# One stream of steps through four attentions, with the first block of the masked attention cut in two by its keys

## The chip, the cores and the metric

The kernel runs on one core of one Trainium2 chip. The metric is the device time of one execution in microseconds (us), lower is better. The profile is of one more execution of the same program.

## The reference

Two transformer layers run one after the other on x, 2048 rows of 256, with 16 heads of 16. The first layer has two attentions and an MLP, the second a masked self-attention, an attention over a context of 1601 rows, and an MLP. Cut to the order of the four attentions:

```python
# layer 0 (mod_*: LayerNorm, then scale and shift), x0, x1 = halves of 1024 rows
x0 = x0 + g * mha(mod(ln(x0)));   x1 = x1 + g * mha(mod(ln(x1)))        # stage 0
ox = attend(q(x0), k(x1), v(x1)); oy = attend(q(x1), k(x0), v(x0))      # stage 1
x = x + g * concat(ox @ w, oy @ w)
x = x + g * gelu_mlp(mod(ln(x)))
# layer 1
x = ln(x + mha(x, x, x, mask))       # stage 2: all 2048 keys, int mask 2048 x 2048
x = ln(x + mha(x, ctx, ctx))         # stage 3: 1601 keys
x = ln(x + relu_mlp(x))
```

Every softmax subtracts the row's maximum. Stage 2 needs keys of every row of x, so of every row that the first layer's MLP has finished.

## The kernel before

**Blocks, groups, units, steps.** The queries are tiled in 4 blocks of 512 rows, the heads in 4 groups of 4. A unit is (stage, block, group): 16 units a stage, 64 in all. The keys of a group lie in two slots (`kT[g][slot]`, `V[g][slot]`), each with half of the keys. Stages 0 and 1 use one slot for a block, stages 2 and 3 both. Blocks go in the order of `ORDER`: 0, 1, 2, 3 in stage 0, and 2, 3, 0, 1 in the others. In stage 2 slot 0 holds the keys of blocks 2 and 3, slot 1 those of blocks 0 and 1.

A unit has two phases. The maxima (`maxima`, L812) multiply queries by keys with queries on the partitions, and VectorE takes row maxima: with one reduction (L827), in stage 2 with two instructions that add the mask and reduce (L820). `negated` and `as_rows` turn the maxima into a row layout (L851, L856). The weights (`weights_of`) compute the transposed scores (L872), add the negated maxima through a small matmul (L879), in stage 2 also the transposed mask (L887), and ScalarE takes the exponential (L892). `values_of` (L908) multiplies by V, whose column of ones gives the sums of the weights. A step is one exponential: 16 a unit in stages 0 and 1, 32 in stage 2, 26 in stage 3.

**The stream.** `stream(stages)` emits all instructions; each engine runs its own in the order of emission. In each step it emits some maxima of the next unit (4 tiles ahead), one pair of values, one step of weights, and then `after(step)`: small tasks from `later` that are due, a mask transpose (`mask_columns`, L780), one key or value transfer from `transfers`, and one advance of the first generator in `background`. At step 2 of a unit, `copy_sums` (L940 to L948) takes the sums of the unit before; `invert` and `divide` (L958 to L973) follow 4 and 8 steps later. When the last group of a block is done, `chain_after` puts the block's chain into `background`, to begin 9 steps on.

**Chains.** `chain_cross(b)` is the longest: projection (L455), LayerNorm, transposes (L339), 8 up products (L509), GELU (L523), 8 down products (L531), transposes, keys (L381), values (L411), queries (L381). Its keys and values go through DRAM, and from there into `kT` and `V` (L701, L715). `chain_context(n)` turns a part of the context into keys and values of stage 3. A generator's piece that needs a PSUM bank is held back in a step in which something in `later` is due or soon will be, or a mask transpose was made or will be made in the next step. `ensure` advances the background generators, with nothing between them, until what is asked for has been emitted.

**The end of stage 1.** The program calls

```python
    stream((0, 1))
    background += [[chain_context(n), 0, False] for n in range(NB)]
    stream((2, 3))
```

The first call finishes the last chain of stage 1, `chain_cross(1)`, with no attention around it, before the second begins with the 32 maxima of its first unit. In that chain the mask of the first masked block is loaded and turned to bf16 (`mask_rows`, L768, L769), in buffers of the tag `w_mlp`.

Of the kernel before, what the change touches and what calls it, by code (L numbers as in the profile page):

```python
# [11 lines left out]
F32 = mybir.dt.float32  # L12
# [39 lines left out]
CTX = ((0, 512), (512, 384), (896, 512), (1408, 193))  # L52
EB = 5
WB = 5
HB = 8
AHEAD = 4
COLUMNS = 6
# [16 lines left out]
def two_layers(ctx: ExitStack, tc: tile.TileContext, a: dict, out: bass.AP):  # L74
# [70 lines left out]
    ident = sb.tile([P, P], F32, tag="ident", name="ident")  # L145
    make_identity(nc, ident)
# [4 lines left out]
    identR = sb.tile([P, P], F32R, tag="identR", name="identR")  # L151
    nc.vector.tensor_copy(identR, ident)
# [103 lines left out]
    cols = sb.tile([P, 48], F32, tag="cols", name="cols")  # L256
    nc.sync.dma_start(cols, a["cols"])
# [327 lines left out]
    def chain_cross(b):  # L585

        last = b == ORDER[1][-1]
        t = residual(x_in(b))
        yield from project(1, b, gated(rows["a1"], t, b))
        if last:  # L590
            load_output(2)
            rows["a2"] = load_rows(7, 3)
        yield 3
        xn = stage([P, TPB, D], name="xn")
        yield from normalize(xn, t, 1e-6)
        hT = yield from transposed(xn, mod=(2, b // 2))

        q0 = ORDER[2][0]
        if last:
            mask_rows(q0, 0)  # L600
        yield from mlp(
            mlp0, 32, AF.Gelu_apprx_tanh, hT, gated(rows["m0"], t, b),
            (lambda: (mask_rows(q0, 1), mask_rows(q0, 2))) if last else None,
        )
        if last:
            mask_rows(q0, 3)
            rows["a3"] = load_rows(10, 3)
        kept((2, b), t)
        yield 3
        hT = yield from transposed(t)  # L610
        yield from keys_and_values(2, hT, b)
        yield from halves(2, 0, hT, b, BLK)
        if last:
            load_attn(3, attn_raw)

# [31 lines left out]
    def chain_last(b):  # L647

        t = residual(xs[3, b])
        yield from project(3, b, biased(rows["a3"], t))  # L650
        yield 3
        yield from post_norm(rows["a3"], t)
        hT = yield from transposed(t)
        yield from mlp(mlp1[0], 40, AF.Relu, hT, biased(rows["m1"], t))
        yield 3
        yield from post_norm(rows["m1"], t)
        nc.sync.dma_start(out[b * BLK : (b + 1) * BLK, :].rearrange("(t p) d -> p t d", p=P), t)
# [29 lines left out]

    waiting: list = []
    transfers: list = []

    def load_keys(st, g, slot):
# [27 lines left out]
        what = (st, g, slot)  # L719
        transfers.extend((what, lambda c=c, i=i: keys(c, i)) for c in range(2) for i in range(4))  # L720
# [37 lines left out]
    def mask_rows(b, qt, quarters=range(NB)):  # L758

        if quarters[0] == 0:  # L760
            t = sb.tile([P, S], BF16, tag="w_mlp", bufs=WB, name="bias")
            blocks.setdefault((2, b), {}).setdefault("bias", []).append(t)
        t = blocks[2, b]["bias"][qt]
        q0 = b * BLK + qt * P
        for j in quarters:
            n = (KEYS[2][0] + KEYS[2][1])[j]
            raw = sb.tile([P, BLK], I32, tag="raw", bufs=2, name="raw")
            nc.sync.dma_start(raw, a["mask"][q0 : q0 + P, n * BLK : (n + 1) * BLK])  # L768
            nc.gpsimd.tensor_scalar(  # L769
                t[:, j * BLK : (j + 1) * BLK], raw, 0.0, MASKED, ALU.is_equal, ALU.mult  # L770
            )

    def mask_columns(b, kt):

        if kt % 2 == 0:
            t = hidden([P, 2, BLK], BF16, name="biasT")
            blocks[2, b].setdefault("biasT", []).append(t)
        m = one_ps(BF16)
        for qt in range(TPB):
            nc.tensor.transpose(  # L780
                m[:, qt * P : (qt + 1) * P],
                blocks[2, b]["bias"][qt][:, kt * P : (kt + 1) * P],
                ident16,
            )
        nc.scalar.copy(blocks[2, b]["biasT"][kt // 2][:, kt % 2, :], m)

    def maxima(u):
# [4 lines left out]
        for slot in slots_of(st, b):  # L792
            nk = slot_rows(st, slot)
            n = -(-nk // BLK)
            size = -(-nk // n)
            size += size % 2
            nk += nk % 2
            chunks += [(slot, c, min(size, nk - c)) for c in range(0, nk, size)]

        def pair(qt, n, i):  # L800
            if "pm" not in u:
                need = [(st, g, slot) for slot in slots_of(st, b)]
                load_ready(need)
                u["pm"] = sb.tile([P, TPB, 2, 2, len(chunks)], F32, tag="pm", bufs=2, name="pm")
            if masked and i == 0:
                at = ORDER[2].index(b)
                if g == NG - 1 and at + 1 < NB:
                    mask_rows(ORDER[2][at + 1], qt, (n,))
# [9 lines left out]
            if masked:  # L818
                for h in range(2):
                    nc.vector.tensor_tensor_reduce(  # L820
                        out=s[:, h, :], in0=s[:, h, :],
                        in1=blocks[2, b]["bias"][qt][:, slot * SLOT + c : slot * SLOT + c + nn],
# [24 lines left out]
    def as_rows(u):  # L847
# [8 lines left out]
        nc.scalar.copy(u["nm"], m)  # L856

    def weights_of(u):
# [5 lines left out]
            for slot in slots_of(st, b) for kt in range(-(-slot_rows(st, slot) // P))  # L864
# [3 lines left out]
        def pair(n, i):  # L868
# [16 lines left out]
            if masked:  # L885
                for h in range(2):
                    nc.tensor.matmul(  # L887
                        s[:, h, :], lhsT=ident16, rhs=blocks[2, b]["biasT"][n // 2][:, n % 2, :],
# [38 lines left out]
    def copy_sums(u):  # L927
# [3 lines left out]
        if g == 0:  # L931
# [6 lines left out]
        oT = blocks[st, b]["oT"]  # L938
        sums = half([P, BLK], name="sums")
        nc.scalar.copy(sums, u["av"])  # L940
        u["weights"] = sb.tile([P, 4 * BLK // P], F32, tag="rd", bufs=4, name="weights")
        for j in range(4):
            nc.sync.dma_start(
                u["weights"][PH * j : PH * (j + 1), :], sums[PH * j + ONE : PH * j + ONE + 1, :]
            )
        for j in range(4):
            at = (g % 2) * (P // 2) + HD * j
            nc.sync.dma_start(oT[at : at + HD, g // 2, :], sums[PH * j : PH * j + HD, :])  # L948

        if st < 3 and b in (ORDER[st][-1], ORDER[st][1]):  # L950
            for slot in slots_of(st, b):
                if st < 2 or b == ORDER[st][-1]:
                    waiting.append((st + 1, g, slot))

    def invert(u):

        rd = sb.tile([P, 4 * BLK // P], F32, tag="rd", bufs=4, name="rd")
        nc.vector.reciprocal(rd, u["weights"])  # L958
        d = dr.tile([4, BLK], F32, tag="rd", bufs=4, name="rd_dr")
        nc.sync.dma_start(d.rearrange("j (p c) -> (j p) c", p=PH), rd)  # L960
        g = u["g"]
        rd_rows = sb.tile([P, BLK], F32, tag="rd_rows", name="rd_rows")
        at = (g % 2) * (P // 2)
        nc.sync.dma_start(
            rd_rows[at : at + P // 2, :], d.unsqueeze(1).to_broadcast([4, HD, BLK])
        )
        u["rd"] = rd_rows[at : at + P // 2, :]

    def divide(u):
# [3 lines left out]
        nc.gpsimd.tensor_tensor(v, v, u["rd"], ALU.mult)  # L973

# [10 lines left out]
    def stream(stages):  # L985

        units = [
            {"st": st, "b": b, "g": g} for st in stages for b in ORDER[st] for g in range(NG)
        ]
        for i, u in enumerate(units):  # L990
            u["i"] = i
            if u["g"] == 0:
                blocks.setdefault((u["st"], u["b"]), {})
        todo = [(u, f) for u in units for f in maxima(u)]
        todo.reverse()

        columns: list = []
        at = 0
        for u in units:
            if u["st"] == 2 and u["g"] == 0:  # L1000
                columns += [(at + 2 * kt - COLUMNS, u["b"], kt) for kt in range(2 * ST)]
            at += 2 * sum(-(-slot_rows(u["st"], s) // P) for s in slots_of(u["st"], u["b"]))
        later: list = []

        def take_maxima():
            if not todo:
                return
            u, f = todo.pop()
            f()
            if not todo or todo[-1][0] is not u:  # L1010
                negated(u)
                later.append([3, lambda: as_rows(u)])
# [7 lines left out]
        def after(step):  # L1020
# [3 lines left out]
            later[:] = [[n - 1, f] for n, f in later if n > 0]  # L1024
            for _, f in due:
                f()
            turned = False
            while columns and columns[0][0] <= step:
                _, b, kt = columns.pop(0)
                mask_columns(b, kt)  # L1030
                turned = True
            load_ready()
            soon = any(n <= 0 for n, _ in later) or (columns and columns[0][0] <= step + 1)
            if background and background[0][1] <= now[0]:
                if not background[0][2] or not (turned or due or soon):
# [6 lines left out]
        first = len(maxima(units[0])) + AHEAD  # L1042
        for n in range(first):
            small[0] = 1
            before()
            take_maxima()
            after(n - first)
        pending: list = []
        step = 0
        for u in units:  # L1050
# [4 lines left out]
            n1 = len(maxima(units[min(i + 1, len(units) - 1)]))  # L1055
            n2 = len(second)
            for s2 in range(n2):
# [3 lines left out]
                if s2 == 6 and i + 2 < len(units):  # L1061
                    load_queries(units[i + 2])
                for _ in range(n1 * (s2 + 1) // n2 - n1 * s2 // n2):
                    take_maxima()
# [11 lines left out]
                if s2 == 2 and i:  # L1076
                    w = units[i - 1]
                    copy_sums(w)
                    later.append([3, lambda w=w: invert(w)])
                    later.append([7, lambda w=w: divide(w)])  # L1080
                    if w["g"] == NG - 1:
# [5 lines left out]
        for _, f in later:  # L1087
            f()
# [20 lines left out]
    stream((0, 1))  # L1109
    background += [[chain_context(n), 0, False] for n in range(NB)]  # L1110
    stream((2, 3))


# [78 lines left out]
```

## Time and profile before

| | us |
|---|---|
| median of 3 runs | 3460.53 (3459.78 to 3466.74) |
| the profiled execution, its own time | 3460.31 |
| its span, first to last instruction | 3458.5 |
| PE busy in the span | 3109.3 (90%) |
| DVE busy | 2122.7 (61%) |
| ACT busy | 1706.6 (49%) |
| POOL busy | 393.9 (11%) |

PE is TensorE, DVE VectorE, ACT ScalarE, POOL GpSimd, SP the engine that issues the DMAs. The profile page shows the span in 40 slices of 86.5 us, a digit being tenths busy; PEclk is the clock granted to TensorE in tenths of full speed. A table by windows gives for each stretch its length, the busy time and the count (x) of each engine, the granted clock, the DMA share and GB/s; limited to one line of the code, it counts that line alone. A group of instructions has its count, its busy time and the mean of one in ns.

### The profile page before, as it was taken

The page shows a single profiled execution, that of the slowest core. Times are in us where ns is not written, and L with a number is a line of the kernel's source. Part 1 is how long each engine was busy: PE and PEld are TensorE (multiplying, and loading weights), DVE is VectorE, ACT ScalarE, POOL GpSimd, SP SyncE. Part 2 cuts the span into 40 slices and gives each one's busy share as a digit, 9 for nine tenths or more (in the row PEclk, how much of TensorE's full clock was granted, in tenths as well). Part 3 has the DMA queues.
Part 4 walks back from the last instruction along what each step waited for, and adds up shares of the span by engine and source line. Part 5 has one row for each costly group of instructions (what it writes and reads, how often), then busy time and mean ns, then how long its engine had stood idle before and what let it go on. Part 6 is the DMA issues. An engine that isn't in the chain of part 4 may idle for free.

```text
span 3458.5 us, 56445 instructions
## 1 busy us (share of the span) xinstructions
PE 3109.3 (90%) x22500; PEld 1368.0 (40%) x22640; DVE 2122.7 (61%) x3808; ACT 1706.6 (49%) x1846; POOL 393.9 (11%) x336
## 2 busy tenths in 40 slices
PE   4899999988989876799999999999998999999995
PEld 2334444433434343343343333333334444444443
DVE  2676766764555411667777767777756756757541
ACT  1365655555454531155555554554555655546461
POOL 0001101101010114002101202201001011110112
PEclk8899999999999997799999999999999999999997
DMA  6652152162112315501001101202123000001000
GB/s 187 147 83 66 47 100 66 55 108 43 51 31 70 67 50 144 112 26 50 20 17 52 45 16 41 55 18 53 35 51 84 20 26 17 25 17 27 18 14 16
DMA packets 155305, 187.34 MB, mean 54 GB/s; under 512 B 77320, under 2 KB 90256, under 8 KB 155040
## 3 DMA queue, kind: packets, MB, share of 16 engines
q1 hardware_dynamic: 155040, 183.71, 22.1%
q8 instruction: 178, 2.92, 0.4%
q14 instruction: 87, 0.71, 0.1%
HBM read 126.78 MB, written 47.90 MB: 51 GB/s over the span
## 4 chain that ended last, share of the span: by engine, by line
PE 75%; DVE 6%; ACT 6%; DMA 6%; issue 2%; SPq 2%; POOL 1%; ACTq 0%; POOLq 0%; DVEq 0%
PE m_ps L908 20%; PE s_ps L872 13%; PE s_ps L812 11%; PE s_ps L879 8%; PE s_ps L887 7%; ACT e L892 4%; PE m_ps L381 3%; PE m_ps L531 3%; PE m_ps L509 3%; DVE pm L827 2%; PE m_ps L455 2%; DMA rd_rows<-rd_dr 2%; DVE s_ps L820 2%; PE m_ps L411 1%; PE m_ps L851 1%
## 5 line engine op out<-in xcount | busy, mean ns | idle before, releaser
L892 ACT ACTIVATE e<-s_ps 128x1024 f32<-128x1024 f32 (+1 forms) x1440 | 1469.8, 1025 | 1323.2 <-PE s_ps L879 799.2
L827 DVE TENSOR_REDUCE pm<-s_ps 128x2 f32<-128x1024 f32 (+3 forms) x1024 | 1119.4, 1106 | 548.8 <-PE s_ps L812 543.5
L908 PE MATMUL m_ps<-e,V 128*32 128x256 f32 (+1 forms) x10496 | 908.0, 416 | 23.3 <-ACT e L892 13.4
L820 DVE CUSTOM_DVE_ANT_0 s_ps<-s_ps,bias 128x512 f32<-128x512 f32 x1024 | 713.8, 700 | 282.4 <-ACT e L892 147.0
L812 PE MATMUL s_ps<-kT,q 64*128 64x512 f32 (+3 forms) x3072 | 684.2, 448 | 112.4 <-ACT e L892 41.0
L872 PE MATMUL s_ps<-q,kT 64*128 64x512 f32 (+1 forms) x2880 | 675.2, 465 | 44.0 <-ACT e L892 22.6
L879 PE MATMUL s_ps<-nm,sel 64*128 64x512 f32 (+1 forms) x2880 | 572.5, 394 | 0.1
L812 PEld LDWEIGHTS s_ps<-kT,q 64*128 64x128 f32 x3072 | 294.8, 188 | 536.8 <-issue 324.8
L872 PEld LDWEIGHTS s_ps<-q,kT 64*128 64x128 f32 (+1 forms) x2880 | 270.0, 184 | 485.9 <-issue 275.0
L908 PEld LDWEIGHTS m_ps<-e,V 128*32 128x32 f32 x10496 | 208.8, 108 | 456.7 <-issue 417.9
L973 POOL TENSOR_TENSOR oT<-oT,rd_rows 64x512 f32<-64x512 f32 x64 | 81.3, 1271 | 1922.5 <-DMA rd_rows<-rd_dr 1388.9
L887 PE MATMUL s_ps<-biasT,ident 128*128 128x512 bf16 x884 | 278.9, 384 | 22.4 <-issue 22.4
L879 PEld LDWEIGHTS s_ps<-nm,sel 64*128 64x128 f32 (+1 forms) x2880 | 274.8, 187 | 9.6 <-ACT nm L856 0.4
L769 POOL TENSOR_SCALAR bias<-raw 128x512 bf16<-128x512 int32 x64 | 123.1, 1924 | 206.5 <-DMA raw<-in_mask 151.7
L820 DVE DVE_READ_ACCUMULATOR2_ANT pm<- 128x1 f32 x1024 | 144.9, 141 | 0.0
L887 PEld LDWEIGHTS <-ident 128*128 128x128 bf16 x1024 | 58.2, 97 | 186.5 <-issue 186.5
L389 DVE SCALAR_TENSOR_TENSOR lo<-m_ps,qkb,hi 128x512 fp32r<-128x512 f32 (+2 forms) x52 | 38.1, 733 | 125.2 <-ACT hi L388 118.8
L381 PE MATMUL m_ps<-hT,w_qk 128*128 128x512 f32 (+2 forms) x208 | 107.8, 644 | 7.7 <-DVE lo L389 6.6
L531 PE MATMUL m_ps<-w_mlp,hid 128*128 128x256 f32 x384 | 100.2, 406 | 0.0
L455 PE MATMUL m_ps<-w_p,oT 128*128 128x256 f32 x224 | 68.7, 449 | 31.6 <-POOL oT L973 31.6
L509 PE MATMUL m_ps<-hT,w_mlp 128*128 128x512 f32 x192 | 95.2, 618 | 0.7 <-ACT hT L354 0.7
L531 PEld LDWEIGHTS m_ps<-w_mlp,hid 128*128 128x128 f32 x384 | 72.0, 197 | 26.8 <-issue 18.3
(98 smaller groups left out, 1250.9 us busy)
## 6 DMA issues: line engine op xcount, KB each, us to landing
q<-q_dr SPq DMA_DIRECT2D x512, 64.0 KB
kT<-k_dr SPq DMA_DIRECT2D x192, 128.0 KB
raw<-in_mask SPq DMA_DIRECT2D x64, 256.0 KB
q_dr<-hi SPq DMA_DIRECT2D x32, 256.0 KB
q_dr<-lo SPq DMA_DIRECT2D x32, 256.0 KB
oT<-sums SPq DMA_DIRECT2D x256, 32.0 KB
rd_rows<-rd_dr SPq DMA_DIRECT2D x64, 128.0 KB
v_dr<-v SPq DMA_DIRECT2D x14, 544.0 KB
```

Of the source, the lines that this page charges most:

```text
L381: nc.tensor.matmul(m[:, :n], lhsT=wqk[:, k, w, c, :], rhs=hT[:, k, :n], start=k == 0, stop=k == 1)
L455: nc.tensor.matmul(y[:, q2, :], lhsT=oT[:, k, qt * P : (qt + 1) * P], rhs=wp[:, k, :], start=k == 0, stop=k == 1,)
L509: nc.tensor.matmul(m, lhsT=w1[k][:, f * P : (f + 1) * P], rhs=hT[:, k, :], start=k == 0, stop=k == 1,)
L531: nc.tensor.matmul(m[:, q2 * D : (q2 + 1) * D], lhsT=hid[f][:, qt * P : (qt + 1) * P], rhs=w2[f // 4][:, f % 4, :], start=f == 0, stop=f = ...
L812: nc.tensor.matmul(s[:, h, :nn], lhsT=u["q"][64 * h : 64 * h + 64, i, qt * P : (qt + 1) * P], rhs=kT[g][slot][64 * h : 64 * h + 64, i, c : ...
L820: nc.vector.tensor_tensor_reduce(out=s[:, h, :], in0=s[:, h, :], in1=blocks[2, b]["bias"][qt][:, slot * SLOT + c : slot * SLOT + c + nn], ...
L827: nc.vector.tensor_reduce(u["pm"][:, qt, :, i, n], s[:, :, :nn], AX.X, ALU.max)
L872: nc.tensor.matmul(s[:r, h, :], lhsT=kT[g][slot][64 * h : 64 * h + 64, i, kt * P : kt * P + r], rhs=u["q"][64 * h : 64 * h + 64, i, :], st ...
L879: nc.tensor.matmul(s[:r, h, :], lhsT=sel[64 * h : 64 * h + 64, i, :r], rhs=u["nm"][64 * h : 64 * h + 64, :], start=False, stop=not masked,)
L887: nc.tensor.matmul(s[:, h, :], lhsT=ident16, rhs=blocks[2, b]["biasT"][n // 2][:, n % 2, :], start=False, stop=True,)
L892: nc.scalar.activation(e[:r], s[:r], AF.Exp, scale=SCALE)
L908: nc.tensor.matmul(u["av"][PH * j : PH * (j + 1), cut], lhsT=V[g][slot][:r, kt * GW + j * VW : kt * GW + j * VW + PH], rhs=u["e"][n, j % 2 ...
```

## The change

There is one call, `stream(range(4))`, and `chain_cross(1)` runs in `background` beside stage 2. The context chains are put into `background` at the end of that chain. Block 2, the first of stage 2 (`SPLIT`), becomes 8 units of 16 steps: four groups with the keys of slot 0 (part 0), then four with those of slot 1 (part 1). Each part has its own maxima and sums. For part 0 the unscaled output goes to DRAM. After a unit of part 1, `compare` takes the larger maximum and two factors by an exponential of 128x32, `invert_both` forms the two scales, and `divide` combines the two outputs on POOL. To compare, each of the 8 units loads its negated maxima back by 8 small DMAs in `as_rows`.

The mask of part 0 lies in the buffers of `kT11` (rows) and `kT21` (columns); so the slot 1 keys of groups 1 and 2 are loaded only when part 0 has done with these. Mask rows are spread over steps by `mask_part`. Maxima have a due step each, 4 steps ahead, at least 0.75 step apart. Of the tasks in `later` only `as_rows` still holds a piece back.

```diff
+SPLIT = ORDER[2][0]
+SPACING = 0.75
...
         yield from mlp(
-            mlp0, 32, AF.Gelu_apprx_tanh, hT, gated(rows["m0"], t, b),
-            (lambda: (mask_rows(q0, 1), mask_rows(q0, 2))) if last else None,
+            mlp0, 0, AF.Gelu_apprx_tanh, hT, gated(rows["m0"], t, b),
+
+            (lambda: mask_part(1)) if last else None,
         )
...
         if last:
             load_attn(3, attn_raw)
+            background.extend([chain_context(n), 0, False] for n in range(NB))
...
+        if st == 2 and slot == 1 and g in (1, 2):
+            kT[g][slot] = sb.tile([P, 2, SLOT], F32R, tag=f"kT{g}{slot}", name="kT")
...
+    def mask_part(slot):
+
+        for n in range(2 * TPB):
+            later.append([n, lambda n=n: mask_rows(SPLIT, slot, n // 2, n % 2), False])
...
         nc.scalar.copy(u["nm"], m)
+        if "part" in u:
+
+            t = sb.tile([P, 2, 4 * BLK // P], F32, tag="mh", bufs=2, name="mh")
+            for j in range(4):
+                for h in range(2):
+                    r = 64 * (j // 2) + 2 * (j % 2) + h
+                    nc.sync.dma_start(
+                        t[PH * j : PH * (j + 1), h, :], u["nm"][r : r + 1, :].bitcast(F32)
+                    )
...
         if st < 3 and b in (ORDER[st][-1], ORDER[st][1]):
-            for slot in slots_of(st, b):
-                if st < 2 or b == ORDER[st][-1]:
-                    waiting.append((st + 1, g, slot))
+            for slot in u["slots"]:
+                if (st == 1 and slot == 1 and g in (1, 2)) or (st == 2 and b != ORDER[st][-1]):
+                    continue
+                waiting.append((st + 1, g, slot))
+        if st == 1 and b == ORDER[1][-1] and g == 1:
+            mask_part(0)
+        if first_part and g == NG - 1:
+            waiting.append((2, 2, 1))
...
+        if u.get("part") == 1:
+            rows_, sums = u["rd_first"], u["first"]
+            nc.gpsimd.tensor_tensor(sums, sums, rows_, ALU.mult)
+            nc.gpsimd.tensor_tensor(v, v, sums, ALU.add)
+
+    def compare(u, w):
...
+        nc.vector.tensor_tensor(both, w["minus"], u["minus"], ALU.min)
+        for i, x in enumerate((w, u)):
+            nc.vector.tensor_tensor(f[:, i, :], both, x["minus"], ALU.subtract)
+        nc.scalar.activation(f, f, AF.Exp, scale=SCALE)
...
+                if (st, b) == (2, SPLIT):
+                    units += [
+                        {"st": st, "b": b, "g": g, "slots": (slot,), "part": slot}
+                        for slot in range(2) for g in range(NG)
+                    ]
...
+        for u, w in zip(reversed(units), [*reversed(units[:-1]), None]):
+            tiles = maxima(u)
+            n = len(tiles)
+            begin, length = (w["start"], w["steps"]) if w else (-n, n)
+            for k in range(n - 1, -1, -1):
+                due = begin + k * length / n - AHEAD
+                todo.append([min(due, todo[-1][0] - SPACING) if todo else due, u, tiles[k]])
...
+            if u.get("part") == 0 and u["g"] == NG - 1:
+                waiting.append((2, 1, 1))
...
-                if not background[0][2] or not (turned or due or soon):
+                if not background[0][2] or not (turned or soon):
...
-                if s2 == 6 and i + 2 < len(units):
+                if s2 == 1 and i + 2 < len(units):
                     load_queries(units[i + 2])
...
+                    elif part == 1:
+                        v = units[i - 1 - NG]
+                        later.append([3, lambda w=w, v=v: compare(w, v), False])
+                        later.append([4, lambda w=w, v=v: invert_both(w, v), False])
+                        later.append([7, lambda w=w: (fetch_first(w), divide(w)), False])
...
-    stream((0, 1))
-    background += [[chain_context(n), 0, False] for n in range(NB)]
-    stream((2, 3))
+    stream(range(4))
```

Beside this, the identity matrix is kept once, as fp32r, and 16 columns of biases are loaded in place of 48.

## Prediction

> **What bounds the kernel now.** First the page's slices:
>
> ```profile
> PE   4899999988989876799999999999998999999995
> DVE  2676766764555411667777767777756756757541
> ...
> PEclk8899999999999997799999999999999999999997
> ```
>
> TensorE is the bound nearly everywhere; in slices 14 to 16 its share falls to 7, 6, 7 and its clock to 0.7. That is the end of stage 1. Then the table by windows limited to L892, with edges at the first exponential of a unit, so that x counts steps:
>
> ```profile
> 603.90:629.10 25.20, 16.18 (x16) 1.00 0.13 33
> 765.70:804.50 38.80, 16.24 (x16) 0.91 0.50 77
> 804.50:838.10 33.60, 16.29 (x16) 1.00 0.10 25
> 838.10:898.30 60.20, 17.59 (x18) 0.94 0.06 17
> 898.30:938.40 40.10, 16.25 (x16) 1.00 0.25 85
> 1066.20:1106.40 40.20, 16.29 (x17) 1.00 0.32 98
> 1240.50:1277.40 36.90, 16.30 (x16) 1.00 0.26 94
> 1277.40:1461.70 184.30, 1.28 (x1) 0.74 0.50 124
> 1603.50:1738.20 134.70, 65.63 (x64) 1.00 0.14 36
> 1738.20:1884.00 145.80, 65.62 (x64) 1.00 0.11 34
> ```
>
> Row 1 is a unit with no chain beside it: 25.2 us. Rows 2 to 5 are the four units of a cross block with a `chain_cross` beside them: 172.7 us. Row 8 is the gap between the two streams: 184.3 us without a step (its x1 is the next unit's first). The last two rows are 64 masked steps without a chain (134.7) and with a `chain_masked` (145.8). The same windows for all engines show what the gap holds and what a masked step is bound by:
>
> ```profile
> 1277.40:1461.70 184.30, 110.19 (x338) 60.99 (x339) 72.66 (x187) 21.80 (x33) 45.99 (x38) 0.74 0.50 124
> 1603.50:1738.20 134.70, 129.92 (x1001) 49.85 (x1020) 98.24 (x267) 69.29 (x71) 25.60 (x14) 1.00 0.14 36
> ```
>
> PE is busy 110 of 184 us at clock 0.74; in masked steps it is busy 96%, DVE 73%. The chain of waits (start, us) says why the gap is long:
>
> ```profile
> 1288.85 1.27 POOL oT L973
> 1304.69 15.07 PE s_ps L509 x30
> 1345.32 3.66 PE s_ps L381 x4
> 1374.42 4.49 DMA kT<-k_dr
> 1378.97 7.52 DMA c<-in_ctx
> ```
>
> One chain goes alone through division, MLP, keys, DRAM and key tiles, and the 32 maxima of the first masked unit then wait for keys and share the queue with the context.
>
> **The change part by part**, against the profiled execution's 3460.3 us, equal to the median (3460.53).
>
> *Removed: 181 us.* The last unit of stage 1 and the gap are 36.9 + 184.3 = 221.2 us. In one stream that unit is like the last unit of the block before, 40.1 us with maxima and the end of a chain. 221.2 - 40.1 = 181.
>
> *Put back: `chain_cross(1)`, in masked steps: 59 us.* Its PE work at full clock, from the chain of waits in stage 1: 8 up products x 1.92, 8 down x 1.93, 4 key and query products x 1.98, 2 values x 1.99, 4 transposes x 0.66 = 45.3; projection 4.9 (group L455 on m_ps: 68.7 us over 14 blocks): 50. Beside it the GELU stops the exponentials (two table loads of 1.28 and 4.27 us), which left PE idle 4.4 us at 1202, and the projection waited up to 5.0 us for the division: 59. A cross block paid more, 172.7 - 4 x 25.2 = 71.9. The masked rows speak for little overhead: a `chain_masked` there costs 145.8 - 134.7 = 11.1 for about 9 of PE work and 16 mask transposes. Bounds 50 and 72.
>
> *Put back: contexts, 28 us.* Three of four lie in the gap: (2 x 0.66 + 2 x 1.98 + 2 x 1.99) = 9.3 us of PE for 512 rows, by size 9.3 + 7 + 9.3 = 25.6; 10% over it, as for the masked chain. Bounds 25 and 37 (the overhead of the cross block, 72/50).
>
> *Moved: first masked maxima.* The 16 tiles of part 0's first unit go beside the last cross unit. A masked tile is 2 x (0.70 + 0.14) = 1.68 us of DVE where an unmasked takes 1.23 there. 16 x 1.68 = 27 stays below the 40 us of that unit, but waits lengthen: 4, bounds 0 and 9. The other 16 replace tiles that the steps already carried.
>
> *Added by the split.* Steps and tiles are as many as before. Four more `as_rows` cost PE 0.66 each and a wait: 4 us, bounds 2 and 10. `compare` and `invert_both` are some ten small DVE operations a unit (the reciprocal takes 0.24): 10 us of DVE in 270, covered by its 27% idle. Two more POOL operations of 1.27 a unit are covered by POOL's idle time. If those covers were gone, 10 and 10 us. Mask rows (16 of 1.92 on POOL, 16 loads) move: part 0's into the last cross block, ahead of divisions on POOL that nothing waits for yet; part 1's just ahead of the last additions of `chain_cross(1)`, which counts below.
>
> *SP's queue.* In a part it carries per unit 8 query loads, 8 of negated maxima, 8 of sums, 2 to 4 of scales and about 10 keys and values: 38. The row: four issues of L943 in 2.44 us, so 0.61 each, one behind another; the sums' 64-byte pieces had landed 1.3 us after the last. So 23 us of a unit's 34 go to issuing, beside the rest. The Trainium skill, "DMA: Bandwidth & Descriptors", section "Anatomy of one DMA", gives each DMA a fixed cost of about 2.0 us (measured there on GpSimd's path) and speaks against 64 more small ones. If that were paid in series, a unit would need 76 us, and eight units would lose over 300. The row shows issues that don't wait for each other's landing; I take it: nothing for issue, with the queue's order as a rival below.
>
> *A new wait at step 44: 26 us.* This is my largest choice. Count steps from the first of part 0. `chain_cross(1)` begins at step 2 + 9 = 11. In the last cross block its twin had its first transposes at step 23, its last up product at 37, the last down product at 46, and its values at about 60 (counted in exponentials of the timeline). Fewer held-back pieces make this 2 to 4 steps earlier: the last down product at 43, the keys above 50. But part 1's first maxima are due at 48 - 4 = 44, and they ask for the keys of block 1. `ensure` then emits the rest of the chain in one piece, and maxima and weights stand behind it in PE's order. After the last down product: additions on DVE and POOL behind the last mask row, 7; two transposes and evacuations 2.5; two key products with hi, lo and a DRAM write between 9; values 5.4; 8 key loads issued 5, landing 4.5. That is 33 us, of which 9 are PE work counted above: 24. The skill's page "TensorE: Matmul & The Clock Gate", Part 1, has the clock fall to half after an idle window of about 3.4 us and stay there for as long after the restart; the gap's 0.74 agrees. So about 1.7 more: 26. Without the rule 24. Bounds 0 (the chain is in time) and 36.
>
> *Late next: 7 us.* At step 60 group 1's keys are asked for, with 2 of 8 loads not yet issued (one per step from 54): 4.5 of landing. At 76 group 2's, whose loads can start only at 67: 0 to 5, so 2.5. Bounds 0 and 15.
>
> Sum: 181 - (59 + 28 + 4 + 4 + 26 + 7) = 181 - 128 = 53; 3460.3 - 53 = 3407. All bounds at once give 105 and 2 us of gain.
>
> **The rivals.** *The chain is in time* (no hole at 44, nor behind it): 53 + 33 = 86 of gain, 3374. For it: maxima ahead of a stage's first key loads never cost more than 4.6 us of PE in stages 0 and 1. Against it: the step count above, 7 or more steps short.
>
> *Chains cost what they cost in a cross block*: 72 for 59, contexts 37 for 28, split 10 for 4, the rest as above: 28 less, 25 of gain, 3435. For it: GELU, evacuations and a single bank per piece are the same. Against it: 11.1 us for a masked chain.
>
> *SP's queue becomes the bound; slower.* SP issues in order, and a DMA that waits for its data holds all behind it: the 8 loads of negated maxima wait for `as_rows`, the sums for ACT, key writes for their evacuation, mask loads for a buffer. With 23 of 34 us of issue a unit has about 10 us for such waits. Beyond that, queries and keys come late and PE stands at each of the eight units. From 53/8 = 6.6 us a unit the gain is gone; at 8 us a unit it ends 11 slower, 3471. Against it: stages 0 and 1 carry 8 + 8 + 2 + 10 issues in units of 25 us without a hole over 5.0 us.
>
> That the change does not do what it says is hardly possible for the gap: the order of emission is fixed, and steps follow the last chain's start. It can only be paid again elsewhere, as above.
>
> **How the numbers follow.** The likeliest, 3407, has 0.50, with a range of its own of 3387 to 3427 (half of the unknown bounds). The chain in time 0.18, cross-block costs 0.22, SP's queue 0.10. About 0.2% (7 us) is what a measurement can tell from no change. All of the first three are faster, 0.90, less 0.02 for their far ends; SP's case gives 0.08 slower and 0.02 within. So 0.88, 0.03, 0.09. For 8 in 10 the range reaches from 3370 (about all of the chain in time) to 3446 (the far side of the cross-block costs), leaving out SP's case and the extremes.
>
> **What would show it.** In the profile after: no window of 100 us without exponentials, and PEclk at 9 or more in slices 14 to 16. A hole on PE of 15 us or more before L812-type maxima that waits for kT<-k_dr, 44 steps into stage 2, with the keys' and values' products of `chain_cross(1)` directly ahead and no exponentials between: right on the largest choice. If these products lie between steps, the rival holds. Part 0's 64 steps should take 135 + 59 + 26, some 220 us, part 1's 135 + 28 + 7, some 170. Stages 0 and 3 should keep their lengths. The prediction is wrong if the eight units show PE waiting for q or kT each time, or if stage 3 starts later than its 53 us of lead says, since contexts pushed `chain_masked` back.

## The result, and the profile after

The changed kernel takes 3405.24 us (median of 4 runs, 3402.13 to 3413.02); the kernel before, beside it, 3460.16 (3456.1 to 3466.74). The ratio is 0.9843, with a 95% interval of 0.9819 to 0.9866: 1.6% faster. The profiled execution took 3407.57 us, its span 3405.8. The forecast was 3407. The sum came out right, two of its parts did not.

In the page's slices after the change (counted from 0), 14 and 15 are back at 9. Slice 16 is still at 7, with the clock at 8: it holds the hole described below. Slices 18 and 19, in part 1, are at 8:

```profile
PE   4899998999999999798899999999999999999995
PEclk8799999999999999899999999999999999999997
```

Then the table by windows, limited to the exponential's line (L941 now), with edges at first exponentials of units. Its rows are the third and fourth unit of the last cross block, part 0 in three stretches (32, 16 and 16 steps), part 1 (64 steps), and the first 64 steps of block 3.

```profile
1169.60:1222.50 52.90, 17.55 (x17) 0.97 0.23 65
1222.50:1265.00 42.50, 16.39 (x16) 1.00 0.23 78
1265.00:1348.60 83.60, 32.79 (x32) 1.00 0.13 33
1348.60:1445.00 96.40, 17.45 (x17) 0.86 0.32 77
1445.00:1492.10 47.10, 16.39 (x16) 0.96 0.58 142
1492.10:1686.80 194.70, 65.52 (x64) 0.93 0.29 78
1686.80:1832.20 145.40, 65.57 (x64) 1.00 0.11 32
```

No stretch is without steps for long. The fourth row is the hole foreseen at step 44: 96.4 us for 16 steps, at clock 0.86. Part 1 takes 194.7 us, where 64 masked steps alone took 134.7.

Set against the kernel before, from the first exponential of each stretch to that of the next (us):

| stretch | before | after | difference |
|---|---|---|---|
| up to the first exponential | 126.0 | 128.6 | +2.6 |
| stage 0 | 503.1 | 510.2 | +7.1 |
| stage 1 up to its last unit | 611.5 | 583.7 | -27.7 |
| last unit of stage 1, with the gap behind it | 221.2 | 42.5 | -178.7 |
| first masked block | 276.5 | 421.7 | +145.2 |
| the other three masked blocks | 834.6 | 834.4 | -0.2 |
| stage 3 and the end | 885.6 | 884.6 | -1.1 |

The single stream and the split earned 178.7 - 145.2 = 33.5 us, not 53. Another 20 came from stages 0 and 1, where I had forecast nothing.

What PE does in part 1, by the table for all engines:

```profile
1492.10:1686.80 194.70, 171.03 (x1110) 71.95 (x1134) 131.46 (x379) 80.15 (x95) 42.77 (x28) 0.93 0.29 78
```

PE is busy 171.0 us, where 64 masked steps alone had 129.9: 41 us more work, at a mean clock of 0.93. It stands for 24 us, where it stood for 5.

The hole itself, from the timeline of ACT and of PE (start, us, engine and line, operation, and in brackets the idle time before it with its releaser):

```profile
1391.22 1.02 ACT L941 ACTIVATE e<-s_ps 128x1024 f32<-128x1024 f32 x1 [2.90 <-PE s_ps L936]
...
1430.69 1.02 ACT L941 ACTIVATE e<-s_ps 128x1024 f32<-128x1024 f32 x1 [20.41 <-PE s_ps L936]
```

```profile
1391.62 1.99 PE L535 MATMUL m_ps<-w_mlp,hid 128*128 128x256 f32 x8
...
1400.30 3.78 PE L385 MATMUL m_ps<-hT,w_qk 128*128 128x512 f32 x4 [0.68 <-ACT hT L358]
1405.71 3.78 PE L385 MATMUL m_ps<-hT,w_qk 128*128 128x512 f32 x4 [1.63 <-DVE lo L393]
1411.12 1.99 PE L415 MATMUL m_ps<-w_v,hT 128*128 128x256 f32 x8 [1.62 <-DVE lo L393]
1413.90 1.99 PE L415 MATMUL m_ps<-w_v,hT 128*128 128x256 f32 x8 [0.78 <-DVE v L425]
1424.32 0.76 PE L843 MATMUL s_ps<-kT,q 64*128 64x512 f32 x1 [8.43 <-issue]
1428.01 0.76 PE L843 MATMUL s_ps<-kT,q 64*128 64x512 f32 x1 [2.93 <-DMA kT<-k_dr]
```

After the last down product (L535) `chain_cross(1)` runs on in one piece, up to its values: transposes, two key products (L385, 3.78 us each where 1.98 is the price at full clock), two value products. Then PE stands for the key tiles. Exponentials stood still from 1391 to 1431. The chain of waits has the landing:

```profile
1420.77 7.11 DMA kT<-k_dr
```

The table by windows for all engines shows the clock, as the last number but two: up to the key products, in them, and behind the hole.

```profile
1393.60:1400.30 6.70, 2.23 (x9) 1.21 (x9) 0.69 (x1) 1.17 (x2) 2.67 (x3) 0.70 0.41 136
1400.30:1411.10 10.80, 7.56 (x8) 2.35 (x8) 1.50 (x2) 1.37 (x2) 0.00 (x0) 0.56 0.13 49
1428.00:1434.00 6.00, 5.66 (x17) 2.35 (x19) 1.51 (x4) 1.02 (x1) 0.00 (x0) 0.52 0.09 19
```

### The profile page after: what moved, and what is told of

It is laid out like the page before. It is cut to its first block, busy times and chain, and to the rows that moved or that the text cites. A ratio compares the mean times of both kernels' runs of the same rounds, so it can differ in the third digit from the quotient of the medians.

```text
span 3405.8 us, 56583 instructions
## 1 busy us (share of the span) xinstructions
PE 3096.5 (91%) x22447; PEld 1359.0 (40%) x22592; DVE 2118.3 (62%) x3858; ACT 1713.7 (50%) x1868; POOL 404.1 (12%) x344
## 4 chain that ended last, share of the span: by engine, by line
PE 75%; DVE 9%; ACT 6%; DMA 4%; issue 2%; SPq 2%; POOL 1%; ACTq 0%; DVEq 0%; POOLq 0%
PE m_ps L957 19%; PE s_ps L921 13%; PE s_ps L843 12%; PE s_ps L928 8%; PE s_ps L936 6%; ACT e L941 5%; PE m_ps L513 3%; DVE pm L858 3%; PE m_ps L535 3%; PE m_ps L385 3%; DVE s_ps L851 2%; PE m_ps L459 2%; PE m_ps L415 2%; PE m_ps L882 1%; DVE t L328 1%
## 5 line engine op out<-in xcount | busy, mean ns | idle before, releaser
L941 ACT ACTIVATE e<-s_ps 128x1024 f32<-128x1024 f32 (+1 forms) x1440 | 1466.9, 1024 | 1376.5 <-PE s_ps L928 791.6
L957 PE MATMUL m_ps<-e,V 128*32 128x256 f32 (+2 forms) x10432 | 903.3, 417 | 15.1 <-ACT e L941 8.0
L957 PEld LDWEIGHTS m_ps<-e,V 128*32 128x32 f32 (+1 forms) x10432 | 207.0, 108 | 439.7 <-issue 412.2
L786 POOL TENSOR_SCALAR bias<-raw 128x512 bf16<-128x512 int32 x64 | 123.0, 1922 | 287.9 <-DMA raw<-in_mask 269.6
L385 PE MATMUL m_ps<-hT,w_qk 128*128 128x512 f32 (+2 forms) x224 | 116.2, 644 | 11.8 <-DVE lo L393 10.7
L535 PE MATMUL m_ps<-w_mlp,hid 128*128 128x256 f32 x448 | 115.1, 401 | 0.0
L513 PE MATMUL m_ps<-hT,w_mlp 128*128 128x512 f32 x224 | 111.0, 618 | 0.7 <-ACT hT L358 0.7
L535 PEld LDWEIGHTS m_ps<-w_mlp,hid 128*128 128x128 f32 x448 | 83.2, 195 | 30.9 <-issue 20.0
L392 ACT ACTIVATE hi<-m_ps,qkb 128x512 fp32r<-128x512 f32 (+2 forms) x56 | 37.8, 674 | 80.8 <-PE m_ps L385 69.2
```

What stands on the lines that cost most here:

```text
L385: nc.tensor.matmul(m[:, :n], lhsT=wqk[:, k, w, c, :], rhs=hT[:, k, :n], start=k == 0, stop=k == 1)
L513: nc.tensor.matmul(m, lhsT=w1[k][:, f * P : (f + 1) * P], rhs=hT[:, k, :], start=k == 0, stop=k == 1,)
L535: nc.tensor.matmul(m[:, q2 * D : (q2 + 1) * D], lhsT=hid[f][:, qt * P : (qt + 1) * P], rhs=w2[f // 4][:, f % 4, :], start=f == 0, stop=f = ...
L786: nc.gpsimd.tensor_scalar(bias_rows[b, slot, qt][:, j * BLK : (j + 1) * BLK], raw, 0.0, MASKED, ALU.is_equal, ALU.mult,)
L941: nc.scalar.activation(e[:r], s[:r], AF.Exp, scale=SCALE)
L957: nc.tensor.matmul(u["av"][PH * j : PH * (j + 1), cut], lhsT=V[g][slot][:r, kt * GW + j * VW : kt * GW + j * VW + PH], rhs=u["e"][n, j % 2 ...
```

## The experiments

Times are medians, with the ratio to the kernel before, run beside it. Lengths of stretches are from one profiled execution of each run. The changed kernel's are 3405.24 and a span of 3405.8. Diffs show the main lines, with `...` for what is left out.

Lengths from one profile scatter. The run "The hold where it helps" changes stages 0 and 3 alone, so its first masked block has the code of the changed kernel. That block took 416.7 us for 421.7: part 0 225.9 for 227.1, part 1 190.8 for 194.7. The part 1 of that run:

```profile
1485.10:1675.94 190.84, 167.08 (x1110) 70.24 (x1126) 130.77 (x379) 80.02 (x95) 42.83 (x28) 0.96 0.30 79
```

It holds the same 1110 products, at clock 0.96 in place of 0.93. So the changed kernel's profile caught a long part 1, and every difference to its 194.7 below may be up to 4 us too large.

**The hole at step 44 taken away: keys of stage 1 in part 1.**

```diff
-        for n in KEYS[st][slot]:
-            ensure(("kv", st, n))
+        old = st == 2 and slot == 1
+        src_st, src_slot = (1, 1) if old else (st, slot)
+        for n in KEYS[src_st][src_slot]:
+            ensure(("kv", src_st, n))
...
-        d = keys_dr[st, slot]
+        d = keys_dr[src_st, src_slot]
...
-            src = values_dr[st, n][:, :, g * GW : (g + 1) * GW]
+            src = values_dr[src_st, n][:, :, g * GW : (g + 1) * GW]
...
-            if w in need or all(("kv", w[0], n) in done for n in KEYS[w[0]][w[2]]):
+            if w in need or w[0::2] == (2, 1) or all(("kv", w[0], n) in done for n in KEYS[w[0]][w[2]]):
```

The last two lines let the loads of these keys start at once, so the run takes away every wait for the keys of part 1, not the hole alone.

> Part 1 of the first masked block takes the keys and values of stage 1 (there since long) in place of its own, so nothing asks for the last chain of stage 1 at step 44; the masked attention is that of other keys. Theory: the hole at step 44 has a price of its own. In the changed kernel exponentials stood still for 39.5 us there, of which about 14 are products of the chain and the step itself; so part 0's third unit falls from 96.3 us to about 71 and the span from 3405.8 to about 3380. Rival: the chain's pieces cost as much when they are spread over steps (waits for evacuations, one bank), so that unit shrinks and the units after it grow by as much: 3400 to 3408.

Measured: 3367.81 us (ratio to before 0.974, 0.9723 to 0.9757), span 3364.1. The windows are part 0 and part 1:

```profile
1270.50:1461.10 190.60, 66.62 (x65) 0.99 0.31 76
1461.10:1651.80 190.70, 65.55 (x64) 0.96 0.32 85
```

Part 0 falls from 227.1 to 190.6, and with part 1 the block falls by 40 us (35 against the block of 416.7). The units behind did not grow: the rival falls. The theory was right in kind; it gave 25 for the hole. Some of part 0's 36 are not the wait: the changed kernel runs the first piece of the contexts there, from step 53, and this run only from step 74. Against the next run, which has no contexts in part 0 either (224.5), the wait costs 34 in part 0. And part 0 without the wait is 56 us above 64 masked steps: that is the price of the whole of `chain_cross(1)` beside masked steps, with the split's bookkeeping.

**Part 1: are the contexts in the way?**

```diff
         if last:
             load_attn(3, attn_raw)
-            background.extend([chain_context(n), 0, False] for n in range(NB))
...
         yield from halves(3, 0, hT, b, BLK)
+        if b == SPLIT:
+            background.extend([chain_context(n), 0, False] for n in range(NB))
```

> The four context chains are put into the background after the masked chain of block 2, so beside block 3's units, not in part 1. Theory: part 1 took 194.6 us where 64 masked steps take 135 and the contexts' products 26; some 25 to 30 us are collisions of the contexts' key splits with SP's queue and the three half buffers there. Block 3's units have half as many small transfers a step: contexts cost about 30 there, part 1 falls to about 145, the span to 3385 to 3392. Rival: contexts cost the same wherever they run: 3402 to 3409.

Measured: 3405.85 us (0.9845, 0.9829 to 0.9861). The first masked block is 30.7 us shorter, the other three are 30.2 longer. The theory falls: contexts cost about 30 us in either place. Part 1 without them is still 166.5 us, 32 above its steps. In it, PE's waits (total, times, longest) have one large entry:

```profile
PE s_ps L844 <- DMA q<-q_dr: 11.4, 2, 11.0
```

The queries of block 3's first unit come late. The timeline of SP shows mask loads (L786) ahead of these queries (L753). Each waits for one of two buffers, and six of them take 12 us:

```profile
1564.56 12.20 SPq L786 DMA_DIRECT2D raw<-in_mask  x6
1576.86 4.14 SPq L753 DMA_DIRECT2D q<-q_dr  x8
```

**The mask loads for block 3, spread.** Part 1's last group has 16 maxima in 12 steps where an unsplit unit has 32 in 32, and the same 16 mask loads hang on them.

```diff
-            if masked and i == 0 and g == NG - 1 and 1 in u["slots"]:
+            if u.get("part") == 1 and i == 0 and g >= NG - 2:
+                k = 8 * (g - 2) + qt * len(chunks) + n
+                mask_rows(ORDER[2][1], k % 4 // 2, k // 4, k % 2)
+            elif masked and i == 0 and g == NG - 1 and 1 in u["slots"] and "part" not in u:
```

> The 16 mask loads for block 3 are issued over the maxima of groups 2 and 3 of part 1, one a tile pair, not all over group 3's. Theory: 16 loads in 12 steps need 16 x 2.4 us (two buffers, 1.92 us of POOL each) where the steps last 25, so SP stands in front of queries and key writes some 13 us; these holes (11.0 us for q in the run with the contexts later, 3.4 + 2.9 + 7.0 for lo in the changed kernel) go: part 1 from 194.6 to about 182, span 3390 to 3396. Rival: the extra maxima in part 1 (16 more tiles than steps) bound it by DVE: part 1 stays above 190, span 3402 to 3408.

Measured: 3401.38 us (0.982, 0.9799 to 0.9841), span 3399.2; part 1 is 185.8 us in place of 194.6. So 5 to 9 us of part 1 depend on how the mask loads are spread (190.8 or 194.7 taken as its length before); by whole times the difference to the changed kernel is not resolved. The rival had part 1 stay above 190, bound by DVE. It took 185.8, so the rival falls for this part. A hole of 7.2 us for `lo` stays: keys are stored as a rounded part `hi` and a remainder `lo`, here for the contexts.

**The buffers of the combination.** In the changed kernel, part 1's largest holes on PE are for `lo`, and DVE, which writes `lo`, waits for POOL. PE's and DVE's waits in part 1:

```profile
PE m_ps L415 <- DVE lo L393: 9.9, 2, 7.0
PE m_ps L385 <- DVE lo L393: 3.4, 1, 3.4
```

```profile
DVE lo L393 <- POOL first L1038: 14.6, 2, 7.9
DVE lo L393 <- DMA k_dr<-hi: 5.8, 1, 5.8
```

`first` and `rd_first`, fetched for the combination, hold two of the three `half` buffers until POOL has used them; `lo` needs one. The run gives them another buffer:

```diff
-        u["rd_first"] = to_rows(u, u["factors"][:, 0, :], half([P, BLK], name="rd_first"))
-        t = half([P, BLK], name="first")
+        two = sb.tile([P, 2, BLK], F32, tag="t", name="firsts")
+        u["rd_first"] = to_rows(u, u["factors"][:, 0, :], two[:, 0, :])
+        t = two[:, 1, :]
```

> The two tiles with which a unit of part 1 fetches the first part's output and scale take a free buffer (tag t) in place of two of the three half buffers, which the key splits of the contexts use. Theory: the waits of lo for POOL's use of first (3.4 and 7.0 us of PE standing, and half clock behind them) go, those for the DRAM writes stay: part 1 from 194.6 to about 184, span 3394 to 3397. Rival: SP's late issue holds lo as long anyway: 3402 to 3408.

Measured: 3399.27 us (0.9825, 0.9808 to 0.9842), span 3396.3; part 1 is 183.0 us, 8 to 12 shorter; by whole times alone the difference is not resolved. DVE's waits for `first` are gone from the trace. PE still waits for `lo` twice, 9.4 us:

```profile
PE m_ps L415 <- DVE lo L393: 9.4, 2, 8.7
```

So the size is that of the theory, but its path is shown in part only: the waits of PE for `lo` fell from 13.3 us to 9.4, and what else `lo` waits for is open.

**The small loads of the negated maxima.** In `as_rows`, the 8 loads are replaced by one memset on POOL. This kernel leaves out the rescaling of the two parts:

```diff
-            for j in range(4):
-                for h in range(2):
-                    r = 64 * (j // 2) + 2 * (j % 2) + h
-                    nc.sync.dma_start(
-                        t[PH * j : PH * (j + 1), h, :], u["nm"][r : r + 1, :].bitcast(F32)
-                    )
+            nc.gpsimd.memset(t, 0.0)
```

> The 64 small loads of the negated maxima are left out and the maxima of both parts taken as equal, so the combination of the two parts has no rescaling. Theory: their issue costs SP about 5 us a unit, which delays what stands behind: 5 to 10 us of the holes in part 1 go, span 3396 to 3401. The prediction's account: nothing, since they are covered, 3402 to 3408. The prediction's rival of SP's queue as the bound: 20 us or more, below 3386.

Measured: 3394.25 us (0.9807, 0.9791 to 0.9823), span 3391.9; part 0 is 4.7 us shorter, part 1 7.3. The median is 11 us below the changed kernel's, and the four times of each don't overlap (3390.82 to 3397.48, and 3402.13 to 3413.02), though the two intervals of the ratio still overlap by a little. So the 64 loads are not covered; in the profiles the block is 7 to 12 us shorter. That is far from the 53 that SP's rival needed to cancel the gain. What stands on SP's queue in part 1 of the changed kernel, by its own waits:

```profile
SPq L752 <- PE s_ps L921: 19.9, 2, 13.0
SPq L1026 <- DVE factors L1061: 19.5, 3, 7.2
SPq L440 <- DVE v L425: 15.8, 4, 8.6
SPq L785 <- POOL bias L786: 12.3, 8, 2.1
```

Query loads that wait up to 13.0 us for a buffer that PE still reads, scales that wait for DVE, context values, mask loads: in SP's timeline the issues stand one behind another, as the queries above behind the mask loads.

**Keys by block.** Maxima of part 1 take block 0's keys first, each block's keys are loaded for themselves, and part 1's mask rows come in the same order:

```diff
                 need = [(st, g, slot) for slot in u["slots"]]
+                if u.get("part") == 1:
+                    need = [(st, g, 1, 0)]
...
+            if u.get("part") == 1 and n == 1 and qt == 0 and i == 0:
+                load_ready([(st, g, 1, 1)])
...
-            for qt in range(TPB) for n in range(len(chunks)) for i in range(2)
+            for qt, n in (
+                [(qt, n) for n in range(len(chunks)) for qt in range(TPB)]
+                if u.get("part") == 1 else
+                [(qt, n) for qt in range(TPB) for n in range(len(chunks))]
+            )
+            for i in range(2)
```

> Part 1's maxima go through block 0's keys first and block 1's after, and keys are loaded by block (twice as many loads of half the size), so that the last chain is asked for at step 52 in place of 44. Theory: the hole is the part of the chain still to come when it is asked for: at 52 the transposes and the first key product are done between steps, what is left is one key product, values, the DRAM write and loads, so the hole falls from about 36 to 20 us; span about 3390. Rival: the price is DRAM and loads whatever is left of the products (about 15 us), and 80 more loads on SP take back the rest: 3400 to 3410.

Measured: 3389.8 us (0.9796, 0.9778 to 0.9813), span 3382.0. Part 0 and part 1:

```profile
1264.00:1462.00 198.00, 66.68 (x65) 0.98 0.27 74
1462.00:1669.50 207.50, 65.61 (x64) 0.93 0.29 81
```

Part 0 is 29 us shorter, more than forecast; part 1 is 13 longer. A part of both is the first piece of the contexts, which here too begins only at step 74. It is 32 loads more, 8 for each of four groups, not 80 as the expectation says. PE's waits over both parts are now for key tiles, at four places:

```profile
PE s_ps L856 <- DMA kT<-k_dr: 20.8, 4, 7.7
```

The hole is cut up and moved. That twice as many loads, issued one per step, come late for the next groups fits this; it was not tried apart. Theory and rival each hold in part, and 16 us of the block remain as gain (11 against 416.7).

**The 20 us of stages 0 and 1.** Two runs undo one small rule each. The first marks `invert` and `divide` as holding pieces back again:

```diff
-                        later.append([3, lambda w=w: invert(w), False])
-                        later.append([7, lambda w=w: divide(w), False])
+                        later.append([3, lambda w=w: invert(w), True])
+                        later.append([7, lambda w=w: divide(w), True])
```

> One part undone: invert and divide again hold back a background piece in the step in which they are due and the step before. Theory: this rule alone made stage 1's units before the last one 27.7 us shorter (611.5 to 583.8), since cross chains run on in fewer steps: here they get it back, stage 1 near 610 and the span about 3425 to 3432. Rival: the queries' earlier loads (step 1 in place of 6) did it: no change here, 3402 to 3409.

Measured: 3406.55 us (0.9845, 0.983 to 0.986). No change in the whole, but not for the rival's reason: stage 1 up to its last unit is 17.3 us longer (601.0) and the first masked block 10 longer (431.8), while the last unit of stage 1 and stage 0 are about 4.5 shorter each and stage 3 is 14.7 shorter (869.9).

The second loads queries at step 6 again in stages 0 and 1:

```diff
-                if s2 == 1 and i + 2 < len(units):
+                if s2 == (6 if u["st"] < 2 else 1) and i + 2 < len(units):
```

> One part undone: in stages 0 and 1 the queries of the unit after next are loaded at step 6 again in place of step 1. Theory: no part in the gain of stage 1, span 3402 to 3409; at most the second units of a block, which grew from 34.0 to 38.2 us, go back to 34 (seven of them: 25 to 30 less, 3378). Rival: the earlier loads made the gain of stage 1: span about 3425 or more.

Measured: 3410.25 us (0.9862, 0.9845 to 0.988). Stage 1 up to its last unit is 10.3 us longer (594.0); the second units of a block keep their 38. Both rules have a share.

**These two rules alone, in the kernel before:**

```diff
-                if not background[0][2] or not (turned or due or soon):
+                if not background[0][2] or not (turned or soon):
...
-                if s2 == 6 and i + 2 < len(units):
+                if s2 == 1 and i + 2 < len(units):
...
-                    later.append([3, lambda w=w: invert(w)])
-                    later.append([7, lambda w=w: divide(w)])
+                    later.append([3, lambda w=w: invert(w), False])
+                    later.append([7, lambda w=w: divide(w), False])
```

> The kernel before with two small parts of the change alone: invert and divide hold back no piece, and queries are loaded at step 1. Two streams, no split. Theory: the 20 us that the changed kernel gained ahead of the gap belong to these two rules (each undone gave back about half of the gain of stages 0 and 1), so stages 0 and 1 up to the last unit fall from 1114.6 to about 1094, the rest stays, span about 3438. Rival: they belong to the due times of the maxima, or need the one stream: 3455 to 3462.

Measured: 3451.07 us (0.9973, 0.9962 to 0.9983). Stages 0 and 1 up to the last unit fall from 1114.6 to 1092.7 (510.3 and 582.4; the changed kernel has 510.2 and 583.7). So the 20 us have nothing to do with the single stream or the split. The whole gained 10 and not 22, since stage 3 grew by 14.4, which the expectation missed.

**The hold where it helps:** the flag is `w["st"] in (0, 3)` in place of `False`.

> invert and divide hold back background pieces again in stages 0 and 3 alone. The run with the hold in all stages was 17 us longer in stage 1, but 4.5 shorter in stage 0 and 14.6 in stage 3. Theory: stages add up, since each is bound by its own steps: stage 3 falls from 884.5 to 870, stage 0 by 4, the span to 3385 to 3390. Rival: stage 3's gain was of another cause (the later state of stage 1's queues): 3400 to 3408.

Measured: 3384.56 us (0.9782, 0.9768 to 0.9797), span 3380.0: stage 3 at 869.9, stage 0 at 505.8, stage 1 at 584.0, as the stages of the other runs said. The rival falls. Over all runs, stage 3 takes 868.2 to 870.1 with the hold (four kernels) and 877.5 to 889.0 in the changed kernel and the seven runs without it: about 13 us in the mean.

**Together:** keys by block, spread mask loads, the other buffer, the hold in stages 0 and 3.

> Together: keys of part 1 by block, mask loads over two groups, first and its scale in tag t, hold in stages 0 and 3. Theory of separate causes: gains against 3405.8 add, 16 for the keys, 9 for the mask loads, 7 for the buffer, 25 for the hold: 3348. Where the mask loads and the buffer cure the same waits: 3355 to 3360.

Measured: 3373.26 us (0.9747, 0.9732 to 0.9763), span 3371.4. This is faster than both kernels by whole times, by 2.5% and 0.9%. It is 11 us or more above both expectations. The hold's gain is there (stage 3 at 868.2). The first masked block is 406.1 us, no better than with keys by block alone (405.5): PE's waits in it are for key tiles again,

```profile
PE s_ps L859 <- DMA kT<-k_dr: 22.9, 4, 9.9
```

So where mask loads and buffers leave room, PE waits for keys, and the gains of part 1 don't add up.

**And with fewer small loads:**

```diff
-            for j in range(4):
-                for h in range(2):
-                    r = 64 * (j // 2) + 2 * (j % 2) + h
-                    nc.sync.dma_start(
-                        t[PH * j : PH * (j + 1), h, :], u["nm"][r : r + 1, :].bitcast(F32)
-                    )
+            for c in range(2):
+                for h in range(2):
+                    r = 64 * c + h
+                    nc.sync.dma_start(
+                        t[64 * c : 64 * c + 64, h, :], u["nm"][r : r + 3 : 2, :].bitcast(F32)
+                    )
```

> As the run of the four together, and the negated maxima are loaded back by 4 DMAs of two rows in place of 8 of one row. Theory: leaving all 8 out gained 12 us, so half of the issues gains about 5 more. Rival: with the mask loads spread SP has room, and it gains nothing (within 3 us).

Measured: 3373.59 us (0.9746, 0.9733 to 0.976). The profiled block is 398.3 us, 8 shorter, but the whole times don't tell the two apart: inconclusive.

## Why the prediction was right, and where it was not

*Removed, 181.* The last cross unit with the gap fell from 221.2 to 42.5: 178.7. Forecast were 181 less 4 for masked maxima, 177. Right.

*`chain_cross(1)` at the rate of masked steps, 59.* Right: 56 with the bookkeeping of part 0, in the run without the wait. The rival of cross-block costs (72 and 10) falls.

*The new wait at step 44, 26, with 7 for later groups.* The mechanism, place and order of events were as written. The size was 34 in part 0, and 40 for the block (35 against the block of 416.7), for 33. The stretch itself was sized well: from the end of the last down product (1393.6) to the first product with the new keys (1428.0) there are 34.4 us, for 33. In it, the key that PE waited for landed 7.1 us after its issue, for 4.5, and the key products with their splits took 10.8, for 9; the additions and transposes took 6.7, for 9.5, since the additions on POOL were not behind mask rows. Less the 9 us of products counted elsewhere, that is 25, so what was short lies behind the hole. The clock is one part: the 6 us there, at 0.52, lost about 3 (an estimate from that clock), and the 1.7 of the prediction was for one stretch of low clock where there were two. The rest is not traced. In the first stretch, PE had stood for at most 2.25 us at a time before the clock fell, less than the idle window of about 3.4 us that the prediction reckoned with, and the clock stayed low from about 1396 to 1410. The two later holes for keys did not show as holes of their own. The rival that the chain is in time falls.

*Contexts, 28.* Right: 30, though a first piece ran in part 0.

*SP's queue and the small work, nothing.* This step failed. Part 1 was to take some 170 us and took 194.7. The prediction priced SP's issues and left out what they stand behind. The runs found three terms in part 1: the small loads cost 3.5 to 7 us there, the bunched mask loads 5 to 9, the buffers that the combination shares with the key splits 8 to 12. They overlap, so they don't add up to a sum, and part of the 25 us stays open. Mask rows were costed only for part 0 and part 1; those of block 3, which the split pushes into 12 steps in place of 32, were missed. So was a count: 16 maxima of the gap are 16 more than the masked steps carried, and not replaced ones. By the profiles, maxima took 32.0 us of PE in 64 masked steps and 38.0 in part 1; what these 6 us cost was not tried alone. SP's rival was right in kind and too large: it needed 6.6 us a unit to cancel the gain.

*Stages 0 and 3 keep their lengths.* Stages 0 and 1 did not: -20.6 together, from two rules of the diff that I had read as details. Stage 3 did in sum only. The two rules together add 14.4 us there in the kernel before; in the changed kernel something gives that back. The maxima's due times also act in that stage; they were not tried alone, so this stays open.

So the total was right by luck: 20 us missed in the split met 20 us missed in stages 0 and 1. (All bounds of the sum at their best give 104 us, not the 105 that the prediction has.)

## What to carry to other kernels

When a serial stretch is moved beside other work, count the steps until its result is asked for: if they are too few, it returns as a hole in the in-order queue. After a split, look at everything that hung on the old unit's steps (loads, masks, buffers): it now comes in fewer of them, here on one issuing queue, where six mask loads stood 12 us ahead of the queries. And read a rule that runs in every stage as an edit of every stage: the same hold cost 17 us in one and saved 15 in another.

## What the runs showed of the hardware that was not expected

Eight small loads of 64-byte pieces, issued in 5 us of SP's time a unit (0.59 us each in the median), were not free beside a busy TensorE: without 64 of them the median was 11 us lower (3394.25 against 3405.24). The key load that PE waited for landed 7.1 us after its issue, where the one read in the gap of the kernel before took 4.5; why was not settled. And in the hole the clock fell to half, and stayed there for some 14 us, though PE stood for at most 2.25 us at a time; in those 14 us PE was busy for two thirds. The same part 1, with the same 1110 products, ran at clock 0.93 in one kernel and at 0.96 in another.
